# Convolution chain, layer 0: the product of transformed frame 0 comes last and is summed onto the accumulator that VectorE has written in PSUM

## The chip, the core and the metric

The kernel runs on one core of a Trainium2 chip. The metric is the device time of one launch, in microseconds; lower is better. TensorE does the matrix products, VectorE (DVE in the profile) and ScalarE (ACT) do elementwise work, SyncE (SP) issues most transfers. Products land in PSUM; everything else lies in SBUF.

## What is computed

`x` has shape (4, 16, 512, 512). Four layers follow one another, each of the form `x = x + f(groupnorm(x))`. Only layer 0 is touched. Its `f` is a pair of blocks, one after the other, of this kind:

```python
def _denoise_block(x, w1, b1, w2, b2, w3, b3, a, b, c):
    trip = _triplets(x)               # frames t-1, t, t+1, mirrored at the ends
    o = a * conv5x5(trip, w1, dilation 1) + b * conv5x5(trip, w2, dilation 2) + c * conv5x5(trip, w3, dilation 4)
    return jnp.tanh(o)
```

Each of the 16 frames of an image is convolved, in three dilations, together with its two neighbours, and the result goes through tanh. The second block works on the first block's output, and `x` is added at the end. Layers 1 to 3 (a 3x3 convolution of quantised input, a box filter, and a 3x3 convolution in the frequency domain) follow.

## The kernel before

**Groups.** Layer 0 takes four output frames at a time. Along the frame axis it uses a fast convolution: out of six neighbouring input frames `d[0]` to `d[5]` VectorE builds six transformed frames `v[0]` to `v[5]` (128 x 2376 elements each, `early` and `late`), TensorE multiplies each with its own transformed weights, and VectorE combines the six products into four output frames. With 4 images, 2 blocks (`conv` 0 and 1, the outputs are named y and z) and 4 groups a block there are 32 groups. I number them 0 to 31: 0 to 3 are block y of image 0, 4 to 7 block z of image 0, 8 to 11 block y of image 1, and so on.

**Slots.** `run` walks through `slot(n, p)`, six slots p = 0 to 5 for each group n. A slot issues one product (`products`, transformed frame `ORDER[p]`), and everything else that is due beside it. The order of instructions on every engine is the order in which the code issues them; nothing is reordered. In a slot: the weights of the next block are loaded on ACT's queue where the block changes (`load_weights`), then the product, then `gather` for the product of the slot before, then tanh of one finished output frame (`activated`), then `late`, the steps that were put off to this slot (`later`, `do`), the write-out of an output frame (`y_out` or `z_out`), `early` for the next group, and the loads (`fetch`, `input_stats`). `transfers` spreads SP's loads and stores of a slot over the slot's matmuls: each waits for a mark in TensorE's stream.

**PSUM.** A product fills one tile[...], and the pool has two such tiles[...]. Products alternate between them: a product can start only when the readers of the product two slots back are done.

**Gather.** Call the product of `v[q]` M_q. In the order of before, (1, 2, 3, 4, 0, 5):

- at slot 1, ACT copies M1 to tile A; at slot 2, DVE makes B = A - M2 and A = A + M2; at slot 3, ACT copies M3 to C;
- at slot 4, DVE makes D = C - M4, C = C + M4, then for each half E = 4 C + A (output 2, through tanh at once) and A = A + C (L575);
- at slot 5, DVE makes A = A + M0 (L579; output 0), then C = 2 D + B (output 1) and B = 8 D + B;
- at slot 0 of the next group, DVE makes B = B + M5 (L579; output 3), and ACT takes tanh of A; at slot 1, ACT takes tanh of B.

All of these are done in two halves of 128 x 1024 elements. Tiles A to E have one buffer each; E has one half only, so the second E can be written when tanh has read the first. Block z reads its halves out of PSUM with a stride of two elements, block y without one. Output tiles of y come from a pool of two (`rb`), those of z from a pool of two (`ra`) that also holds the normalised input `xp`.

Of the kernel before, what the change touches and what calls it, by code (L numbers as in the profile page):

```python
# [13 lines left out]
F32 = mybir.dt.float32  # L14
AF = mybir.ActivationFunctionType
# [5 lines left out]
P = 128  # L21
B, C, H, W = 4, 16, 512, 512
# [8 lines left out]
DELTA = (-4, -2, -1, 0, 1, 2, 4)  # L31
NPB = 2 * len(DELTA)
NQ = 6
ORDER = (1, 2, 3, 4, 0, 5)
KN = 9 * 264
NFRAMES = 10
AFTER = mybir.DependencyInfo(mybir.DependencyClass.Sync, mybir.DependencyReason.SCHED_ONLY)
# [83 lines left out]
class Layer0:  # L121
# [148 lines left out]
    def first(self):  # L270
# [12 lines left out]
        self.weights()  # L283
        for q in ORDER:
            self.load_weights(0, q)
# [226 lines left out]

    def products(self, gr, p):
        nc, conv, q = self.nc, gr["conv"], ORDER[p]
        ps = self.psum.tile([P, 4, 512], F32, name=f"m{self.now}", tag="m")
        v = gr["v"][q].rearrange("p (k r) -> p k r", r=264 if conv else 72)
        w = self.w[q].rearrange("p (n o) -> p n o", o=PX)
        for n in range(NPB):
            e, dr = n // len(DELTA), DELTA[n % len(DELTA)]
            for turn in range(16):  # L520
                i, j = turn // 4, turn % 4
                rows = slice(PX * i, PX * i + PX)
                r0 = 4 + dr + (64 * j if conv else 0)
                k0 = e + (0 if conv else 8 * j)
                ins = nc.tensor.matmul(  # L525
                    ps[PX * j : PX * j + PX, i, :].rearrange("p (k r) -> p k r", r=64),
                    w[rows, n],
                    v[rows, k0 : k0 + 8, r0 : r0 + 64],
                    start=(n == 0),
                    stop=(n == NPB - 1),  # L530
                    skip_group_check=True,
                )
            self.marks.append(ins.ins)
        gr["m"][q] = ps

    def gather(self, gr, p):

        nc, conv = self.nc, gr["conv"]
        m = gr["m"].pop(ORDER[p])
        s = gr.setdefault("s", {})  # L540

        def new(tag):
            shape = [P, 1024] if tag == "E" else [P, 2, 1024]
            return self.pools["sum"].tile(shape, F32, name=f"{tag}{self.now}", tag=tag)

        def part(h):

            if conv:
                return m.rearrange("p c (k r) -> p (c k) r", r=64)[:, :, h::2]
            return m.rearrange("p c n -> p (c n)")[:, 1024 * h : 1024 * h + 1024]  # L550

        def of(t):
            return t.rearrange("p (k r) -> p k r", r=32) if conv else t

        if p in (0, 2):
            t = s["A" if p == 0 else "C"] = new("A" if p == 0 else "C")
            for h in range(2):
                nc.scalar.copy(of(t[:, h]), part(h))  # L558
        elif p == 1:
            s["B"] = new("B")  # L560
            for h in range(2):
                nc.vector.tensor_sub(of(s["B"][:, h]), of(s["A"][:, h]), part(h))
                nc.vector.tensor_add(of(s["A"][:, h]), of(s["A"][:, h]), part(h))
        elif p == 3:
            s["D"] = new("D")
            for h in range(2):
                c, d = (s[t][:, h] for t in "CD")
                nc.vector.tensor_sub(of(d), of(c), part(h))
                nc.vector.tensor_add(of(c), of(c), part(h))
            for h in range(2):  # L570
                a, c = (s[t][:, h] for t in "AC")
                e = new("E")
                self.stt(e, c, 4.0, a)
                self.activated(gr, 2, h, e)
                nc.vector.tensor_add(a, a, c)  # L575
        else:
            t = s["A" if p == 4 else "B"]
            for h in range(2):
                nc.vector.tensor_add(of(t[:, h]), of(t[:, h]), part(h))  # L579
            for h in range(2) if p == 4 else ():  # L580
                b_, c, d = (s[t][:, h] for t in "BCD")
                self.stt(c, d, 2.0, b_)
                self.stt(b_, d, 8.0, b_)


    def activated(self, gr, i, h, src):

        nc, conv = self.nc, gr["conv"]
        name = f"{gr['b']}_{conv}_{4 * gr['g'] + i}_{h}"
        bias = self.biases[:, conv : conv + 1]  # L590
        if conv:
            z = self.pools["ra"].tile([P, 1024], F32, name=f"z_{name}", tag="ra")
            nc.scalar.activation(z, src, AF.Tanh, bias=bias)
            gr["out"][i, h] = z
        else:
            if h == 0:
                gr["out"][i, 0] = self.pools["rb"].tile([P, 8, 264], F32, name=f"y_{name}", tag="rb")
            z = gr["out"][i, 0]
            o = z[:, :, 4 + 128 * h : 132 + 128 * h].rearrange("p k (c r) -> p c k r", c=2)
            nc.scalar.activation(o, src.rearrange("p (c k r) -> p c k r", c=2, k=8), AF.Tanh, bias=bias)  # L600
            to, even, odd = (
                (z[:, :, 0:4], z[:, :, 8:4:-1], z[:, :, 7:3:-1])
                if h == 0
                else (z[:, :, 260:264], z[:, :, 259:255:-1], z[:, :, 258:254:-1])
            )
            nc.scalar.mul(to, even, self.parity[:, 0:1])
            gr["rim"].append((to, odd))
# [60 lines left out]
    def slot(self, n, p):  # L668

        self.now, self.moves = 6 * n + p, {"first": [], "loads": [], "stores": []}  # L670
        self.marks = []
        groups = self.groups
        cur = groups[n] if 0 <= n < len(groups) else None
        nxt = groups[n + 1] if n + 1 < len(groups) else None
        last = groups[n - 1] if n > 0 else None
        self.last_of_image = (n - 7) % 8 < 2
        if cur:
            if p == 0 and cur["g"] == 0:
                self.begin(cur)
            for i in range(2):  # L680

                if nxt and nxt["g"] and i + 4 in cur["d"]:
                    nxt["d"].setdefault(i, cur["d"][i + 4])

        done, at = (cur, p - 1) if p else (last, 5)
        if done:
            self.free.append(done["v"].pop(ORDER[at]))
            after = nxt if p else cur
            if after and after["conv"] != done["conv"]:
                self.load_weights(after["conv"], ORDER[at])  # L690
        if cur:
            self.products(cur, p)
        if done:
            self.gather(done, at)


        for i, at in enumerate((6, 5, 4, 7)):
            of = cur if p >= 4 or p == 3 and i == 2 else last
            early = of and of["g"] < 3 and i != 3
            if of and of["conv"] and p == (at - early) % 6:  # L700
                of["xb"][i] = [self.load_x(of["b"], 4 * of["g"] + i, h, "xb") for h in range(2)]
        of, i = {4: (cur, 2), 5: (cur, 1), 0: (last, 0), 1: (last, 3)}.get(p, (None, 0))
        if of and i != 2:
            src = of["s"]["CAB"[(1, 0, 3).index(i)]]
            for h in range(2):
                self.activated(of, i, h, src[:, h])
        if cur:
            self.late(cur, p)
        self.do("rows")
        if of:  # L710
            (self.z_out if of["conv"] else self.y_out)(of, i)
        self.do("rest")
        self.do("last")
        if nxt:
            step = p - (3 if nxt["conv"] == 0 and nxt["g"] == 0 else 2)
            if step in (0, 1):
                self.early(nxt, step)
            self.fetch(nxt, p)
        if cur and cur["conv"] == 0 and cur["b"] + 1 < B and p >= 2:
            self.input_stats(cur["b"] + 1, 4 * cur["g"] + p - 2)  # L720
# [66 lines left out]
class Kernel:  # L787
# [594 lines left out]
    def layer3(self, x3, sums, gn, l3, out):  # L1382
# [3 lines left out]
        with ExitStack() as ctx:  # L1386
# [196 lines left out]
            with tc.manual_schedule():  # L1583
# [17 lines left out]
                rows(0)  # L1601
                spread(0)
                products(0)
                imaginary(0)
                load(2)
# [8 lines left out]
                next(edge)  # L1614
                scalars(0)
                products(1)
                next(edge)
                masked(1)
# [101 lines left out]
```

## Time and profile before

| | us |
|---|---|
| median of 3 runs | 5329.93 (5324.8 to 5330.24) |
| the profiled execution | 5314.9 |
| its span | 5313.1 |
| granted TensorE clock, mean of the span | 0.982 |
| layer 0's products (L525), first to last | 74.4 to 3026.6 |

The profiled execution took 1.8 us more than its span, and was 15.0 us faster than the median. The views used are: the page (busy time of each engine, and the span in 40 slices), the groups of instructions by line, the waits (who waited for whom), and the timeline, in which a row has start, duration, engine, line, operation, output and inputs, and in brackets the idle time of the engine before it with what ended it. The profile has 86,016 matmul records in L525. That is 448 for each of the 192 slots, so the start of every 448th record is the start of a slot; slot times below are found that way. The shortest slot takes 14.18 us, the mean one 15.38 us.

### The profile page before, as it was taken

How to read it: one execution, taken by the hardware profiler on the slowest of the kernel's cores; microseconds unless marked ns; L12 is line 12 of the kernel's file. 1: busy time of each engine (PE TensorE's matmuls, PEld its weight loads, DVE VectorE, ACT ScalarE, POOL GpSimd, SP SyncE). 2: the span in 40 equal slices, each digit the busy share in tenths (PEclk: the TensorE clock that was granted, in tenths of full speed). 3: DMA queues.
4: the chain of work that ended last, by engine and by line, in shares of the span. 5: the costliest groups of instructions: out<-in, count | busy, mean ns of one | idle time of the engine just before them, and what ended most of it. 6: DMA issues, size and time to landing. Idle time of an engine off the chain costs nothing.

```text
span 5313.1 us, 270477 instructions
## 1 busy us (share of the span) xinstructions
PE 5014.8 (94%) x125040; PEld 3651.4 (69%) x125040; DVE 4034.6 (76%) x4764; ACT 2491.1 (47%) x3954; POOL 6.8 (0%) x20
## 2 busy tenths in 40 slices
PE   4999998999999999989999789998999989999999
PEld 3676676766776856758766655566887867777776
DVE  7867989768988669987689855555555578888887
ACT  2543445533255533444122445554454446666665
POOL 0000000000000000000000000000000000000000
PEclk9999999999999999999999999999999989999999
DMA  5555554555545455543346377776666655555554
GB/s 170 170 145 157 144 156 148 161 148 137 143 152 169 139 160 137 150 134 117 103 128 153 126 222 231 234 238 202 225 222 199 214 158 143 144 149 148 143 143 121
DMA packets 445356, 861.49 MB, mean 162 GB/s; under 512 B 74304, under 2 KB 96704, under 8 KB 443968
## 3 DMA queue, kind: packets, MB, share of 16 engines
q1 hardware_dynamic: 415792, 797.68, 51.8%
q10 hardware_dynamic: 28432, 46.52, 2.7%
q8 instruction: 979, 16.04, 1.4%
q14 instruction: 153, 1.25, 0.1%
HBM read 503.87 MB, written 340.03 MB: 159 GB/s over the span
## 4 chain that ended last, share of the span: by engine, by line
PE 89%; DVE 6%; issue 2%; DMA 2%; ACT 1%; SPq 0%; ACTq 0%; POOL 0%; DVEq 0%; POOLq 0%
PE m L525 51%; PE l1p L975 10%; PE l2p L1082 8%; PE u L1550 4%; PE s L1491 4%; PE u L1491 4%; PE u L1513 2%; PE pt L1525 2%; DVE l2o L1122 2%; PE l2p L1133 1%; DVE st L1123 1%; DVE frame L441 0%; PE pr L1535 0%; ACT xp L377 0%; DVE zr L627 0%
## 5 line engine op out<-in xcount | busy, mean ns | idle before, releaser
L525 PE MATMUL m<-frame,l0w 32*32 32x512 f32 x86016 | 2856.1, 604 | 170.5 <-DVE frame L481 74.4
L525 PEld LDWEIGHTS m<-frame,l0w 32*32 32x32 f32 x86016 | 2073.7, 103 | 952.0 <-issue 363.1
L441 DVE SCALAR_TENSOR_TENSOR frame<-frame,frame 128x2376 f32<-128x2376 f32 x232 | 607.9, 2629 | 9.2 <-DMA xs<-in_x 0.8
L975 PE MATMUL l1p<-l1q,l_wt 32*32 32x512 f32 x12288 | 482.6, 600 | 61.3 <-DVE l1q L965 35.7
L975 PEld LDWEIGHTS l1p<-l1q,l_wt 32*32 32x32 f32 x12288 | 258.3, 103 | 231.6 <-issue 155.4
L1122 DVE TENSOR_TENSOR l2o<-l2x,l2p 128x512 f32<-128x512 f32 x256 | 172.7, 675 | 270.4 <-PE l2p L1082 270.4
L652 ACT ACTIVATE junk<-xb,neg 128x1024 f32<-128x1024 f32 x256 | 294.2, 1149 | 62.1 <-DMA l0w<-l0w 32.9
L1082 PEld LDWEIGHTS l2p<-k_c_band,l2y 128*128 128x128 f32 x2048 | 256.8, 190 | 76.0 <-issue 55.2
L1082 PE MATMUL l2p<-k_c_band,l2y 128*128 128x144 f32 (+1 forms) x2048 | 284.3, 292 | 6.1
L1082 PE MATMUL l2p<-k_c_band,l2n 128*128 128x144 f32 (+1 forms) x2048 | 272.5, 294 | 14.4 <-ACT l2n L1100 10.9
L1111 ACT COPY l2y<-l2p 128x512 f32<-128x512 f32 x256 | 149.9, 586 | 286.9 <-PE l2p L1082 286.9
L1082 PEld LDWEIGHTS l2p<-k_c_band,l2n 128*128 128x128 f32 x2048 | 265.8, 199 | 15.3 <-ACT l2n L1100 11.4
L992 DVE BATCH_NORM_STATS2 l1st<-l1o 128x6 f32<-128x512 f32 x256 | 158.2, 681 | 140.3 <-ACT l1o L990 140.3
L990 ACT ACTIVATE l1o<-l1p,k_l_bias,l_osc 128x1024 f32<-128x1024 f32 x128 | 147.2, 1201 | 240.1 <-PE l1p L975 234.2
L1550 PE MATMUL u<-k_c_hil,zt 128*128 128x128 f32 x2048 | 255.9, 278 | 0.0
L558 ACT COPY C<-m 128x1024 f32<-128x1024 f32 x64 | 61.6, 1014 | 405.9 <-PE m L525 317.6
L1550 PEld LDWEIGHTS u<-k_c_hil,zt 128*128 128x128 f32 x2048 | 238.4, 192 | 2.1 <-issue 0.8
L405 DVE STREAM_TRANSPOSE frame<-xp 128x1056 f32<-128x1056 f32 x128 | 162.8, 1282 | 90.5 <-ACT xp L379 90.4
L1526 ACT COPY zt<-pt 128x512 f32<-128x512 f32 x256 | 131.4, 599 | 207.8 <-PE pt L1525 207.8
L1456 DVE TENSOR_TENSOR xc<-l3n,k_c_tab 128x2048 f32<-128x2048 f32 x64 | 146.7, 2292 | 108.1 <-ACT l3n L1440 108.1
L1569 DVE SCALAR_TENSOR_TENSOR l3o<-u,l3t 128x256 f32<-128x256 f32 x512 | 192.3, 427 | 22.3 <-ACT l3t L1561 19.5
L975 PE MATMUL l1p<-l1x,l_wt 32*32 32x512 f32 x4088 | 196.7, 597 | 0.0
(309 smaller groups left out, 6376.9 us busy)
## 6 DMA issues: line engine op xcount, KB each, us to landing
y<-y SPq DMA_DIRECT2D x256, 264.0 KB
frame<-y SPq DMA_DIRECT2D x512, 132.0 KB
x<-l1o SPq DMA_DIRECT2D x256, 256.0 KB
l2x<-x SPq DMA_DIRECT2D x64, 1024.0 KB
x<-l2o SPq DMA_DIRECT2D x64, 1024.0 KB
l3x<-x SPq DMA_DIRECT2D x256, 256.0 KB
out<-l3o SPq DMA_DIRECT2D x256, 256.0 KB
l1x<-x SPq DMA_DIRECT2D x252, 256.0 KB
```

Source lines behind the costliest of these rows:

```text
L405: nc.vector.transpose(v[:, :, 4 + h : 68 : 2], xp)
L441: self.nc.vector.scalar_tensor_tensor(o, x, f, y, ALU.mult, ALU.add)
L525: ins = nc.tensor.matmul(ps[PX * j : PX * j + PX, i, :].rearrange("p (k r) -> p k r", r=64), w[rows, n], v[rows, k0 : k0 + 8, r0 : r0 + 64 ...
L652: nc.scalar.activation(junk, xs[h], f, bias=neg, accum_out=self.out_sums[n][:, 2 * t + h : 2 * t + h + 1])
L975: ins = nc.tensor.matmul(ps[32 * j : 32 * j + 32, b, :], wt[rows, a, d], qs[v % 3][rows, k, d : d + W] if d < 3 else raws[v][rows, k], sta ...
L992: nc.vector.bn_stats(st[b][:, u, :], o[:, b, :])
L1082: nc.tensor.matmul(ps[:, lo:hi], lhs[:, k, at : at + P], band[:, j : j + hi - lo], start=(k == 0), stop=(k == 3), skip_group_check=True,)
L1111: nc.scalar.copy(yts[i][:, wb, :], ps)
L1122: nc.vector.tensor_add(o[:, hb, :], xt[:, hb, :], ps)
L1491: nc.tensor.matmul(ps[b][32 * j : 32 * j + 32], f[rows, n, j, :], x[rows, j, :], start=(i == 0), stop=(i == 2 and tag == "s"), skip_group_ ...
L1550: nc.tensor.matmul(po[:, bass.ts(k, P)], zt[:, b, k ^ 1, :], hil[:, k, :], start=False, stop=(k == 3), skip_group_check=True,)
L1569: nc.vector.scalar_tensor_tensor(o[:, v].rearrange("p k u -> p u k"), po[:, HW:W].rearrange("p (u k) -> p u k", u=2), s, t.rearrange("p (u ...
```

## The change

Frame 0 and frame 5 change places: the order is (1, 2, 3, 4, 5, 0).

- At slot 4, a PSUM tile `base` is taken (the one that M4 has just been read from), and DVE writes A + C into it, both halves, before the two E steps. The SBUF-only step A = A + C goes.
- At slot 5, TensorE adds the product of `v[0]` to that tile: no matmul of this product has `start`. DVE gathers M5 in this slot, for each half after C = 2 D + B and B = 8 D + B.
- At slot 0 of the next group DVE gathers nothing. ACT takes tanh of output 0 straight from PSUM.

```diff
-ORDER = (1, 2, 3, 4, 0, 5)
+ORDER = (1, 2, 3, 4, 5, 0)
...
-        ps = self.psum.tile([P, 4, 512], F32, name=f"m{self.now}", tag="m")
+
+        ps = gr.pop("base") if q == 0 else self.psum.tile([P, 4, 512], F32, name=f"m{self.now}", tag="m")
...
-                    start=(n == 0),
+                    start=(n == 0 and q != 0),
...
-        def part(h):
+        def part(h, m=m):
...
+            base = gr["base"] = self.psum.tile([P, 4, 512], F32, name=f"m{self.now + 1}", tag="m")
+            for h in range(2):
+                a, c = (s[t][:, h] for t in "AC")
+                nc.vector.tensor_add(part(h, base), of(a), of(c))
             for h in range(2):
                 a, c = (s[t][:, h] for t in "AC")
                 e = new("E")
                 self.stt(e, c, 4.0, a)
                 self.activated(gr, 2, h, e)
-                nc.vector.tensor_add(a, a, c)
-        else:
-            t = s["A" if p == 4 else "B"]
+        elif p == 4:
             for h in range(2):
-                nc.vector.tensor_add(of(t[:, h]), of(t[:, h]), part(h))
-            for h in range(2) if p == 4 else ():
                 b_, c, d = (s[t][:, h] for t in "BCD")
                 self.stt(c, d, 2.0, b_)
                 self.stt(b_, d, 8.0, b_)
+                nc.vector.tensor_add(of(b_), of(b_), part(h))
+        else:
+            s["M"] = [part(h) for h in range(2)]
...
-            nc.scalar.activation(z, src, AF.Tanh, bias=bias)
+            to = z.rearrange("p (k r) -> p k r", r=32) if i == 0 else z
+            nc.scalar.activation(to, src, AF.Tanh, bias=bias)
...
-            src = of["s"]["CAB"[(1, 0, 3).index(i)]]
+            src = of["s"]["CMB"[(1, 0, 3).index(i)]]
             for h in range(2):
-                self.activated(of, i, h, src[:, h])
+                self.activated(of, i, h, src[h] if i == 0 else src[:, h])
```

## The prediction

> **What bounds the kernel now.** I read the page first, then the waits of TensorE inside layer 0, then DVE's groups, then the timeline at the slots where TensorE waits.
>
> ```profile
> PE 5014.8 (94%) x125040; PEld 3651.4 (69%) x125040; DVE 4034.6 (76%) x4764; ACT 2491.1 (47%) x3954; POOL 6.8 (0%) x20
> ...
> PE   4999998999999999989999789998999989999999
> ...
> DVE  7867989768988669987689855555555578888887
> ```
>
> ```profile
> PE m L525 <- DVE frame L481: 74.4, 1, 74.4
> PE m L525 <- issue: 68.7, 40, 10.8
> PE m L525 <- ACT C L558: 13.0, 5, 5.4
> PE m L525 <- DVE frame L441: 9.3, 5, 4.4
> PE m L525 <- PE m L525: 3.4, 5, 0.9
> ```
>
> TensorE bounds layer 0: its row is nines from slice 2 on, and after the first 74.4 us it waits only 94.4 us in total (68.7 + 13.0 + 9.3 + 3.4). That is the most that lighter DVE work could give back. In its 2953 us DVE is busy for 2400, so work taken from it counts only where TensorE is waiting for it.
>
> ```profile
> L575 DVE TENSOR_TENSOR A<-A,C 128x1024 f32<-128x1024 f32 x64 | 78.4, 1225 | 2.2
> ...
> L568 DVE TENSOR_TENSOR D<-C,m 128x1024 f32<-128x1024 f32 x64 | 77.8, 1215 | 17.3 <-PE m L525 17.3
> ...
> L579 DVE TENSOR_TENSOR B<-B,m 128x1024 f32<-128x1024 f32 x62 | 72.5, 1210 | 39.0 <-PE m L525 38.9
> ```
>
> These are the steps that the change drops, turns into PSUM writes, or moves. The timelines show where DVE holds TensorE (DVE's rows, then TensorE's):
>
> ```profile
> 808.74 2.34 DVE L579 TENSOR_TENSOR A<-A,m 128x1024 f32<-128x1024 f32 x2
> ...
> 826.17 2.31 DVE L579 TENSOR_TENSOR B<-B,m 128x1024 f32<-128x1024 f32 x2
> ...
> 866.55 2.63 DVE L441 SCALAR_TENSOR_TENSOR frame<-frame,frame 128x2376 f32<-128x2376 f32 x1
> ...
> 899.93 1.22 DVE L569 TENSOR_TENSOR C<-C,m 128x1024 f32<-128x1024 f32 x1
> ```
>
> ```profile
> 811.18 1.17 PE L525 MATMUL m<-frame,l0w 32*32 32x512 f32 x16 [4.71 <-issue]
> ...
> 869.28 5.32 PE L525 MATMUL m<-frame,l0w 32*32 32x512 f32 x102 [10.52 <-issue]
> ...
> 901.26 19.35 PE L525 MATMUL m<-frame,l0w 32*32 32x512 f32 x592 [0.95 <-PE m L525]
> ```
>
> The waits marked "issue" are DVE's in truth. TensorE goes on at 811.18, 0.10 us after A + M0 has ended (group 7, so group 8 can start); at 869.28, 0.10 us after frame `v[4]` of group 8; at 901.26, 0.11 us after the last C + M4 of group 8, which frees the tile for slot 5. From 780 to 905 us, between two images, DVE has hardly a gap. The same places return in images 2 and 3.
>
> ```profile
> 1420.26 0.01 DVE L433 LOAD_MASK_SELECT frame<-frame  x1 [3.13 <-DMA frame<-y]
> ...
> 1438.01 1.22 DVE L569 TENSOR_TENSOR C<-C,m 128x1024 f32<-128x1024 f32 x1
> 1439.15 1.22 DVE L441 SCALAR_TENSOR_TENSOR E<-C,A 128x1024 f32<-128x1024 f32 x1
> 1440.40 1.22 DVE L575 TENSOR_TENSOR A<-A,C 128x1024 f32<-128x1024 f32 x1
> 1441.59 1.23 DVE L441 SCALAR_TENSOR_TENSOR E<-C,A 128x1024 f32<-128x1024 f32 x1
> ```
>
> This is slot 4 of group 14, in the middle of an image. The slot began at 1424.3; DVE came to C + M4 so late because in slot 3 it had waited for a load, not because it had too much to do. It ends at 1439.23, and slot 5 starts at 1439.45: a margin of 0.2 us.
>
> **The change part by part.**
>
> DVE's sum. A = A + C becomes the write of `base`: two steps for two. No row shows a DVE write to PSUM. The nearest are SBUF to SBUF (1225 ns, L575) and PSUM read (1215 ns, L568), the latter with z's stride and without it alike (L562: 9.69 us for the 8 steps of block z of image 0, 9.71 for those of block y of image 1), so the read side costs nothing. [...] I take 1225 ns, 2.45 us for both[...]. B = B + M5 moves from slot 0 to slot 5, and A = A + M0 is gone: 2 x 1.21 = 2.43 us less for a group, 78 us over 32. But E has one half. In before, A + C (1.23 us) lay between the two E steps and covered tanh of the first (1.15 us). Now the second E waits for tanh: about 1.2 us of idle DVE for a group. Net: some 1.2 us less for a z group, and about nothing for a y group, where the second rim step also waits for a tanh that A + C had covered.
>
> New wait at slot 5. TensorE's slot 5 needed the last C + M4; now it needs `base` 2.45 us later. Queued behind the waiting matmul is all of TensorE. Taking for each group the time from the end of C to the start of slot 5, most have 3 us or more and pay nothing. These do not: group 0 (0.10), 8, 16, 24 (0.10 each), 13 (1.78), 14 (0.20), 21 (1.35), 22 (1.62), 27 (0.23), 30 (2.45), and 7, 15, 23 (0.10). The price is 2.45 + 0.10 less the margin. Groups 13, 14, 21, 22, 30: 0.77 + 2.35 + 1.20 + 0.93 + 0.10 = 5.35 us. Group 27: 2.32 us. DVE was late there because of a load, as in the lines above, so the step saved at slot 0 earns no credit: 7.7 us.
>
> Between the images. Group 7: slot 5 starts 2.3 us later. Then the release of M5's tile comes after C, B, add, C, B, add (7.3 us) instead of after two adds (2.34), and the E wait puts DVE 1.1 us later: group 8 starts near 817.2 instead of 811.2. Next, slot 1 of group 8 needs the tile that tanh of output 0 reads; ACT ended that in before at 833.95, 5.4 us after the slot had begun, and I get 835.3 against 828.6. So TensorE is 6.7 us late here. It does not last: slot 3 of group 8 is set by DVE's frame at 869.18, and slots 1 and 2 end by 864.6. DVE's own chain there is +1.2 - 2.3 with a little ACT: 0.9 us earlier. SP's loads are tied to marks of TensorE, but at 836 to 871 SP is behind those marks already, held by buffers. At slot 5 of group 8 the `base` steps add 2.45; the 0.9 comes off if it passes ScalarE's wait for an input load at 870 us (0.72 us). I take 2.0 us a boundary, three times: 6.0 us.
>
> First group: slot 5 waits 2.45 us more, group 1's first two slots shift by more, and the frame that ends at 218.6 collects it; going down DVE's rows with the input statistics and the y store in between I get 1.6 us.
>
> Last group. B + M5 (2.35 us from 3026.61) goes from between the last product and layer 1, and tanh of output 0 (2.17 us) runs beside DVE's output steps: 2.35 us less.
>
> Restart. [...] This case: after waits of 5 us and more, and after one of 2.52 (773.57), the next slot has two steps of 0.74 us at matmuls 16 and 32 and costs 1.4 us; after others of 2.51 and 3.1 it doesn't. [...] I take one, 1.4 us.
>
> At nothing: tanh from PSUM (ACT's copy from PSUM takes 1014 ns, tanh from SBUF 1150; if it were slower, ACT is idle several us in every slot). Tile use of slot 1: outside group 0 and the boundaries tanh of output 0 ended 3.7 us or more before it. Release for slot 0: its margin is 5 us or more against some 6, of which slot 5's own delay gives back the rest. Weight loads on ACT's queue and frames freed keep their slots. If these covers were gone, each would cost the shortfall, under 2 us a place.
>
> Sum: 7.7 + 6.0 + 1.6 - 2.35 + 1.4 = 14.3 us; 5314.9 becomes 5329.2, and the median 5329.93 becomes 5344.
>
> **The rivals.** A measurement of this kernel can tell about 0.2%, 10.7 us, from no change.
>
> Absorbed: TensorE's short gaps inside slots (some 130 us above 14.2 us a slot outside the slot borders) shrink after a stall, and half of the new waits vanish: about 5334. For it: those gaps are irregular. Against: nothing shows that a stall fills them.
>
> Boundary not absorbed: SP's loads do follow the 6.7 us, and slot 3 of group 8 with them. 3 x 6.7 on top gives 5364. It decides once SP is no longer behind the marks.
>
> Relief counts: DVE is the bound between images, the dropped add (2.43 us) goes through to slot 5 of groups 8, 16 and 24, cancels `base` there and shortens three boundaries, the start and the end; and `base` finds slack. 5 x 2.4 = 12 us less: 5318. For it: DVE's unbroken rows from 780 to 905. Against: margins of 0.1 to 0.2 us at slot 5, and the E wait. It decides only if DVE's lateness at slot 4 is carried over from slot 0; the 3.13 us wait for a load says no.
>
> [...]
>
> **How the numbers follow.** New wait, 5344: 0.50, of which 0.10 falls inside the bound; not absorbed 0.16; absorbed 0.24; relief 0.10. Slower 0.40 + 0.16 = 0.56, same 0.34, faster 0.10. The range, 5328 to 5363, takes in absorbed, most of the slower case and the unknown write price; the likeliest case's own is 5337 to 5353.
>
> **What would show it.** `base` near 1.22 us a half; the second E waiting about 1.2 us for tanh; TensorE waiting for `base` at slot 5 of groups 14 and 27; group 8 starting some 6 us later and its slot 3 at the same place or earlier; the last product about 15 us later, and layer 1 some 2 us closer to it. Slot 3 of group 8 several us earlier, or no wait at slot 5, would prove me wrong.

## The result, and the profile after

| | before | after |
|---|---|---|
| median of 5 runs, us | 5329.93 (5324.8 to 5330.24) | 5350.48 (5341.12 to 5357.6) |
| profiled execution, us | 5314.9 | 5341.12 |
| its span, us | 5313.1 | 5339.3 |
| granted TensorE clock, mean | 0.982 | 0.98 |

The ratio is 1.0043, 95% interval 1.0028 to 1.0058: 20.5 us slower by the medians, where the prediction said 14.3. Both profiles are fast draws, before's by 15.0 us under its median and after's by 9.4, so their difference of 26.2 us is some 6 too large. A second session with the same kernel (below) gave 1.0040 [1.0023, 1.0057].

First the page of after, busy time and slices:

```profile
PE 5022.7 (94%) x125040; PEld 3689.4 (69%) x125040; DVE 3970.0 (74%) x4700; ACT 2485.1 (47%) x3954; POOL 6.9 (0%) x20
...
PE   4999998999999999989999889998999989999999
...
DVE  7866979767888858988578856555555578888887
```

DVE has 64 instructions and 64.6 us less to do; TensorE has as many instructions as before (125,040). The groups of DVE say what the new step and E cost (total, duration of one in ns, then the idle time before them):

```profile
L574 DVE TENSOR_TENSOR m<-A,C 128x1024 f32<-128x1024 f32 x64 | 78.9, 1233 | 2.2
L441 DVE SCALAR_TENSOR_TENSOR E<-C,A 128x1024 f32<-128x1024 f32 x64 | 78.2, 1222 | 38.9 <-ACT y L605 19.5 <-ACT z L598 19.4
```

The write of `base` (L574) takes 1233 ns a half. The second E waits 38.9 us in 32 groups, 1.22 each: that is what the dropped A = A + C had covered.

TensorE's waits inside layer 0 (engine and line, who was waited for; us in total, times, longest):

```profile
PE m L526 <- DVE frame L481: 74.9, 1, 74.9
PE m L526 <- issue: 67.8, 44, 8.0
PE m L526 <- DVE m L574: 17.9, 6, 4.4
PE m L526 <- ACT C L559: 17.5, 6, 5.1
PE m L526 <- ACT y L605: 4.4, 1, 4.4
PE m L526 <- ACT z L598: 3.2, 3, 1.6
PE m L526 <- DVE frame L441: 1.3, 1, 1.3
```

After the first wait these are 112.1 us, against 94.4 before. The row "DVE m L574" is new: six waits for `base`. It does not hold all of the waits for `base`: some still stand under "issue". Here is one from the new row, in the middle of an image, at slot 5 of group 5 (DVE's rows, then TensorE's):

```profile
613.58 1.22 DVE L570 TENSOR_TENSOR C<-C,m 128x1024 f32<-128x1024 f32 x1
614.83 2.50 DVE L574 TENSOR_TENSOR m<-A,C 128x1024 f32<-128x1024 f32 x2
617.24 1.22 DVE L441 SCALAR_TENSOR_TENSOR E<-C,A 128x1024 f32<-128x1024 f32 x1
619.67 1.23 DVE L441 SCALAR_TENSOR_TENSOR E<-C,A 128x1024 f32<-128x1024 f32 x1 [1.22 <-ACT z L598]
```

```profile
599.45 14.19 PE L526 MATMUL m<-frame,l0w 32*32 32x512 f32 x415
617.48 28.12 PE L526 MATMUL m<-frame,l0w 32*32 32x512 f32 x783 [3.84 <-DVE m L574]
```

The last C ends at 614.80. In before no later step stands in the way of slot 5; now TensorE goes at 617.48, 0.15 us after `base` (614.83 + 2.50).

Between images 0 and 1, TensorE in the timeline of after (slot 5 of group 7, slot 0 of group 8, slots 1 and 2; then slot 3, and slot 5 of group 8):

```profile
806.54 17.03 PE L526 MATMUL m<-frame,l0w 32*32 32x512 f32 x448 [4.42 <-DVE m L574]
831.14 16.78 PE L526 MATMUL m<-frame,l0w 32*32 32x512 f32 x448 [7.57 <-issue]
848.93 29.67 PE L526 MATMUL m<-frame,l0w 32*32 32x512 f32 x896 [1.01 <-ACT z L598]
882.19 10.12 PE L526 MATMUL m<-frame,l0w 32*32 32x512 f32 x244 [3.59 <-issue]
...
918.68 31.91 PE L526 MATMUL m<-frame,l0w 32*32 32x512 f32 x916 [3.56 <-issue]
```

TensorE's lag behind before, read slot by slot, each kernel counted from its own first matmul, is 12.9 us when slot 4 of group 7 starts, 15.7 at its slot 5, 19.5 when group 8 starts, 12.4 at its slot 3 (where before waited 10.5 us for the frame, and after 3.6), 16.9 at its slot 5, and 19.1 when group 9 starts. Most of this growth lies in waits. The last part, 2.2 us, is no wait: slot 5 of group 8 itself takes 16.39 us instead of 14.23. The windows of time show why. First before, in the first 3.4 us of slot 5 of groups 7 and 8, then after at the same two slots (window, its length, PE busy and matmuls, granted clock, DMA share, GB/s):

```profile
790.40:793.80 3.40, 3.40 (x109) 1.00 0.90 209
901.26:904.66 3.40, 3.40 (x111) 1.00 0.14 39
```

```profile
806.54:809.94 3.40, 3.40 (x65) 0.50 0.06 22
918.68:922.08 3.40, 3.40 (x65) 0.50 0.00 0
```

After waits of 4.4 and 3.6 us the clock is granted at 0.50, and 65 matmuls are issued in the time of 110. I call this a slow start, or a restart. A slot that starts so is over a microsecond longer, beyond the wait itself.

### The profile page after: what moved, and what is told of

The parts are those of the page before. It is cut to its first block, busy times and chain, and to the rows that moved or that the text cites. A ratio compares the mean times of both kernels' runs of the same rounds, so it can differ in the third digit from the quotient of the medians.

```text
span 5339.3 us, 270467 instructions
## 1 busy us (share of the span) xinstructions
PE 5022.7 (94%) x125040; PEld 3689.4 (69%) x125040; DVE 3970.0 (74%) x4700; ACT 2485.1 (47%) x3954; POOL 6.9 (0%) x20
## 4 chain that ended last, share of the span: by engine, by line
PE 86%; DVE 7%; issue 2%; DMA 2%; ACT 2%; SPq 0%; ACTq 0%; DVEq 0%; POOL 0%; POOLq 0%
PE m L526 49%; PE l1p L980 10%; PE l2p L1087 7%; PE u L1555 4%; PE s L1496 4%; PE u L1496 4%; PE u L1518 2%; PE pt L1530 2%; DVE l2o L1127 2%; PE l2p L1138 1%; DVE frame L441 1%; DVE st L1128 1%; ACT xp L377 0%; PE pr L1540 0%; DVE frame L481 0%
## 5 line engine op out<-in xcount | busy, mean ns | idle before, releaser
L526 PEld LDWEIGHTS m<-frame,l0w 32*32 32x32 f32 x86016 | 2118.3, 103 | 937.1 <-issue 368.3
L1087 PE MATMUL l2p<-k_c_band,l2n 128*128 128x144 f32 (+1 forms) x2048 | 267.8, 291 | 14.0 <-ACT l2n L1105 10.5
L441 DVE SCALAR_TENSOR_TENSOR y<-y,k_c_parity 128x32 f32<-128x32 f32 x128 | 30.5, 249 | 260.7 <-ACT y L611 222.5
```

What stands on the lines that cost most here:

```text
L441: self.nc.vector.scalar_tensor_tensor(o, x, f, y, ALU.mult, ALU.add)
L526: ins = nc.tensor.matmul(ps[PX * j : PX * j + PX, i, :].rearrange("p (k r) -> p k r", r=64), w[rows, n], v[rows, k0 : k0 + 8, r0 : r0 + 64 ...
L1087: nc.tensor.matmul(ps[:, lo:hi], lhs[:, k, at : at + P], band[:, j : j + hi - lo], start=(k == 0), stop=(k == 3), skip_group_check=True,)
```

## What a wait costs beside itself

All 14 profiles of this case together (before, after and the twelve experiments) have 2674 slot starts. I sorted them by the gap from the start of the last matmul of one slot to the start of the first of the next (some 0.6 us more than the idle time in a row's brackets), and measured the time of the first 64 matmuls. The last column counts the slots in which the granted clock was below full speed during these 64:

| gap before the slot, us | slots | first 64 matmuls, median us | slots over 2.8 us | slots with a lowered clock |
|---|---|---|---|---|
| under 1 | 2296 | 2.09 | 51 | 0 |
| 1 to 2 | 84 | 1.77 | 0 | 1 |
| 2 to 3 | 77 | 2.14 | 25 | 41 |
| 3 to 4 | 60 | 2.92 | 32 | 51 |
| over 4 | 157 | 3.38 | 147 | 157 |

A gap of over 4 us costs 1.3 us more, nearly always; one of 2 to 4 us does so in 57 of 137 cases; one of 1 to 2 us does not. The 204 slow starts behind gaps of over 1 us ran at a mean clock of 0.50 to 0.60. The 51 slots over 2.8 us behind gaps under 1 us ran at full clock, so they have another cause and are not counted below.

In the traces the same wait costs a restart in one execution and none in the next, and this goes with where the wait falls. In each of the 14 profiles all stretches at half clock in layer 0, 12 to 24 of them (12 in before and 21 in after, the one in front of layer 1 counted), start on one grid of 3.413 us, to within 5 ns, and where this grid lies against the kernel's start differs from execution to execution. The clock was lowered behind none of the 98 gaps of over 1 us that cover less than 1.7 us of any one step of this grid, behind 34 of the 63 that cover 1.7 to 2.2 us, and behind 216 of the 217 that cover more. A gap of 2 to 4 us can fall on either side of that.

Slow starts behind gaps of over 1 us number 9 in before and 17 in after, and together they cost 11.2 and 20.2 us over the 2.09. So the account of the lag at the end of layer 0, 29.2 us, is: gaps between slots 95.3 to 115.4, +20.1; slow starts +9.0; the rest, inside slots, +0.1. In the repeated run it is 24.3 us: gaps +24.0, slow starts +11.7 (19 of them), rest -11.4. The rest scatters between executions of whatever kernel, so that it came to 0.1 in the first profile is chance. Before itself has only one profile: 9 is one draw. Layer 1 then takes back 3.2 us (4.9 in the repeat), as its own first wait shows, before and then after:

```profile
3062.24 1.88 PE L975 MATMUL l1p<-l1q,l_wt 32*32 32x512 f32 x2 [35.67 <-DVE l1q L965]
```

```profile
3088.68 1.88 PE L980 MATMUL l1p<-l1q,l_wt 32*32 32x512 f32 x2 [32.44 <-DVE l1q L970]
```

## Experiments

Each session timed its kernels beside before on one chip; chips differ between sessions. Ratios are to before; medians differ by some tenths of a per cent between sessions (before's lie between 5299.94 and 5333.45), so only ratios and differences in one session count, and a difference in us is given as the ratio's share of before's median. The same holds for the absolute times in the expectations: they start from before at 5330. Edits are shortened; "..." stands for lines left out. "Slot-5 waits" are the gaps before slot 5 summed over the 25 groups away from the image ends (0, 7, 8, 15, 16, 23 and 24 left out); in before they are 0, in after 9.3 us.

**The order alone.** Frame 0 last and M5 gathered early, but no seed (no sum that is written into PSUM ahead of the product): A = A + C stays in SBUF and DVE adds M0 at slot 0. The edit is against after.

```diff
+    start=(n == 0)
...
-    base = gr["base"] = self.psum.tile(...)
-    for h in range(2):
-        nc.vector.tensor_add(part(h, base), of(a), of(c))
...
+        nc.vector.tensor_add(a, a, c)
...
-            s["M"] = [part(h) for h in range(2)]
+            nc.vector.tensor_add(of(A), of(A), part(h))
```

> The new order of the six products stays, and so does the late gather of M5 (C, B, add for each half), but nothing is seeded in PSUM: A = A + C is made in SBUF in its old place, M0 goes to a tile of its own and VectorE adds it to A at slot 0. Theory 1 (the cost is the write of base that stands between the gather of M4 and slot 5): slot 5 again waits for C + M4 only, so about 5330 us, at most 5 us more for the later release of M5's tile. Rival (the new order itself, with the later release before slot 0): it keeps its cost, about 5350 us.

Measured: 5328.24 against 5321.69, ratio 1.0009 [0.9997, 1.0021]. Slot-5 waits 2.3 us. The order costs some 5 us, not told from nothing: most of the loss lies in the seed.

**The write alone.** Before, with `base` written into slot 5's tile (here that of M5), and then overwritten because this product keeps its `start`.

```diff
+    base = gr["base"] = self.psum.tile(...)
+    for h in range(2):
+        nc.vector.tensor_add(part(h, base), of(a), of(c))
...
+    ps = gr.pop("base") if p == 5 else self.psum.tile(...)
```

> The kernel before, with one thing added: after the gather of M4, VectorE writes A + C into the PSUM tile of slot 5's product, which then overwrites it (its first matmuls have start). Order, gather, tanh and everything else are those of before; VectorE has 2.46 us more work for a group. Theory 1: the wait at slot 5 is all there is to it, so some 15 to 22 us more than before, 5345 to 5352 us. Rival (late release, second E step waiting for tanh): neither is here, so 5330 us, or as much more as 2.46 us of VectorE work cost between the images (three times, 7 us).

Measured: 5360.87 against 5321.69, ratio 1.0077 [1.0059, 1.0095]: +41 us, twice what I expected. Gaps between slots are 27.4 us more than before (slot 5 in mid-image groups 17.6, the groups at the image ends 10.5), and slow starts 16 instead of 9 (+8.3 us). Two of its waits, the second in front of layer 1:

```profile
PE m L525 <- issue: 92.3, 51, 10.7
PE l1p L979 <- DVE l1q L969: 37.8, 1, 37.8
```

It is also some 19 us slower than after (1.0043 and 1.0040; the intervals just miss each other), although the same write stands in front of slot 5. The difference is what after saves: A = A + C and A = A + M0, 4.9 us of DVE a group, less the E wait, with the order changed besides. Where these steps count can be seen. From the start of group 7 to that of group 9, and likewise at the other two image boundaries, this kernel falls 22.2 us further behind before, after only 14.3 (12.9 in the repeat). At slot 3 of groups 8, 16 and 24 it is still 3.0 to 4.1 us late, where after is between 2.3 us early and 0.5 late. And layer 1's wait is 2.1 us longer than in before, where after's is 3.2 shorter. So after's +21 us is a net: a larger cost at slot 5, less a relief of DVE at the image ends.

**Both, so that the place differs.** After with A = A + C kept (its result unused), one step behind each E.

```diff
     self.activated(gr, 2, h, e)
+    nc.vector.tensor_add(a, a, c)
```

> The changed kernel, with A = A + C left in its old place behind each E step (its result is used by nobody). VectorE has 2.45 us more work for a group, as much as before the change, of which 1.2 us fill the idle time at the second E step. Theory 1: relief of VectorE is worth next to nothing, so 5350 us, at most 4 us more (1.2 us at three boundaries). Rival (the relief does earn some 10 us, which the wait at slot 5 hides): about 5360 us.

Measured: 5350.27, ratio 1.0051 [1.0033, 1.0068], +27 us. DVE has as many steps a group here as in the order-alone kernel, and the E steps don't wait (idle before them 0.0). Between the two, +5 and +27, lie 22 us for having two of these steps in front of slot 5 instead of behind it. To after (+21) the difference is within the intervals, so this run does not decide between the two expectations for the relief (20 to 24 us over before, or 30).

**The write twice.** After with `base` written two times.

```diff
     for h in range(2):
         nc.vector.tensor_add(part(h, base), of(a), of(c))
+    for h in range(2):
+        nc.vector.tensor_add(part(h, base), of(a), of(c))
```

> The changed kernel, with base written twice over (four steps instead of two, the same values). Slot 5 can start 2.46 us later. Theory 1, by the margins of the changed kernel: the twelve groups that wait for base outside the last group of an image (0, 5, 6, 8, 13, 14, 16, 21, 22, 24, 27, 29) pay 2.46 us more each, 29.5 us, and the eight y groups with 0.7 to 1.1 us of margin left (1, 2, 9, 10, 17, 18, 25, 26) begin to pay 1.4 to 1.8 us each, 12 us: some 40 us more than the changed kernel, 5380 to 5395 us. Rival (VectorE's total load or the late release): 2.46 us more for a group between the images only, 5355 to 5360 us.

Measured: 5380.09 against 5302.0, ratio 1.0143 [1.0126, 1.0161]: +76 us, 55 over after in the same session. The waits of TensorE:

```profile
PE m L526 <- DVE frame L481: 75.4, 1, 75.4
PE m L526 <- issue: 74.4, 37, 9.4
PE m L526 <- DVE m L577: 57.8, 20, 6.8
```

The row of `base` goes from 6 waits to 20, and slot-5 waits in mid-image groups from 17.7 us (repeat) to 52.2. All eight y groups that were named beforehand (1, 2, 9, 10, 17, 18, 25 and 26) now wait, by gaps of 1.3 to 1.9 us where 1.4 to 1.8 were expected. The path is confirmed. The second write cost 55 us where some 40 were expected. It saves nothing, so it stands beside the 41 of the write alone, and not beside after's net of 21; whether it costs more than the first, the intervals don't tell.

**After once more**, in the same session.

> The changed kernel once more, on the chip of the two others, to compare them with it: 5345 to 5355 us.

Measured: 5321.66 against 5302.0, ratio 1.0040 [1.0023, 1.0057]. Slot-5 waits in mid-image groups were 17.7 us in this profile, in groups 5, 13, 14, 21, 22, 29 and 30; in the first profile 9.3, in 5, 6, 21 and 22.

**Filling slot 4.** After with C = 2 D + B and B = 8 D + B taken from slot 5 to slot 4, behind each E, so that they cover the wait for tanh and M5's tile is free after two adds.

```diff
     self.activated(gr, 2, h, e)
-elif p == 4:
-    for h in range(2):
         b_, c, d = (s[t][:, h] for t in "BCD")
         self.stt(c, d, 2.0, b_)
         self.stt(b_, d, 8.0, b_)
-        nc.vector.tensor_add(of(b_), of(b_), part(h))
+elif p == 4:
+    for h in range(2):
+        nc.vector.tensor_add(of(s["B"][:, h]), of(s["B"][:, h]), part(h))
```

> The changed kernel, with C = 2 D + B and B = 8 D + B moved up into slot 4, each right behind the E step of its half. The second E step no longer leaves VectorE idle for 1.2 us, and the gather of M5 is two adds, so its tile comes free 4.9 us earlier than in the changed kernel. The write of base is where it was. Theory 1: slot 5 waits as in the changed kernel; group 8 and its like start about 5 us earlier, which slot 3 takes back; the idle time saved is worth at most 1.2 us a boundary. About 5345 us, 5340 to 5351. Rival (late release and idle E step are the cost): about 5330 us.

Measured: 5329.92 against 5321.69, ratio 1.0020 [1.0010, 1.0030], +11 us. The 5330 that the rival named is met only as an absolute time, in a session in which before took 5321.69; as a difference, the theory gave 10 to 21 us and the rival none, so +11 lies at the theory's lower end and off the rival. The idle time before E is gone:

```profile
L441 DVE SCALAR_TENSOR_TENSOR E<-C,A 128x1024 f32<-128x1024 f32 x64 | 78.0, 1219 | 0.0
```

Two more kernels split the edit, and it was repeated beside them. In the first the same steps stand behind both E steps, so E still waits; in the second only the first half's C = 2 D + B stands between the E steps, so M5's tile is still released late.

```diff
     for h in range(2):
         self.stt(e, c, 4.0, a)
         self.activated(gr, 2, h, e)
+    for h in range(2):
+        self.stt(c, d, 2.0, b_)
+        self.stt(b_, d, 8.0, b_)
...
```

> The changed kernel with the two C and two B steps of a group (4.9 us of DVE) taken from behind the products of frame 5 to the end of slot 4, behind both E steps: M5's tile is released after two adds again, but the second E still waits about 1.2 us for tanh. e3_fill, where the same steps lay between the two E steps, cost +10.6 us against before, the changed kernel +21. If the late release made the difference: as e3_fill, +8 to +13 us (about 5332). If the idle 1.2 us in each group made it: near the changed kernel, +17 to +22 us.

```diff
     self.activated(gr, 2, h, e)
+    if h == 0:
+        self.stt(c, d, 2.0, b_)
...
```

> The changed kernel with only the first half's C step moved between the two E steps, so that the wait of the second E for tanh is covered, while the release of M5's tile still comes after five steps (B, add, C, B, add; 6.1 us instead of 7.3). If the idle E step made the difference between e3_fill and the changed kernel: +9 to +13 us against before. If the late release made it: +17 to +22 us. If both count for half: about +15 us.

> e3_fill once more, beside the two kernels that split its edit: the ratio to before was 1.0020 [1.0010, 1.0030]. Both theories expect the same again, 1.001 to 1.003, that is +5 to +16 us; in its second profile the waits of TensorE at slot 5 in mid-image groups (1.7 us in the first) should stay under 5 us if filling slot 4 takes them away.

Measured against 5299.94 in one session: early release 5319.55, 1.0039 [1.0028, 1.0050]; wait filled 5316.9, 1.0037 [1.0024, 1.0049]; both together again 5314.16, 1.0026 [1.0015, 1.0036]. Each half was expected to bring the +11 if it was the cause, and neither shows a gain alone over after's 1.0040. Both together gave 1.0020 and 1.0026; some 7 to 11 us of after's cost may lie there, but the intervals touch, and which of the two does it stays open. The slot-5 waits of the filled kernel were 2.1 us in the first profile and 15.0 in the second, so the reading of the first one, that filling slot 4 takes them away, was the draw of one execution.

**The seed only in the last group of a block z** (7, 15, 23, 31), with the filled slot 4; all other groups as before.

```diff
+SEEDED = (1, 2, 3, 4, 5, 0)
...
-    {"b": b, "conv": conv, "g": g, ...}
+    {"order": SEEDED if conv and g == 3 else ORDER, "b": b, "conv": conv, "g": g, ...}
```

> A version meant to keep the gain and drop the cost: only the last group of block z of each image (groups 7, 15, 23, 31) has the new order and the seed, with C and B moved up behind the E steps; the other 28 groups are those of before. In those four groups the wait at slot 5 is taken back by slot 3 of the next group (or falls before layer 1). Theory 1: no new wait that lasts, VectorE 2.4 us earlier at slot 3 of groups 8, 16 and 24 where slot 5 of that group doesn't give it back, and the last product 2 to 3 us closer to layer 1: 5320 to 5328 us. Rival (the relief never passes ScalarE's waits between the images): 5327 to 5331 us, the same as before.

Measured: 5298.11 against 5302.0, ratio 0.9986 [0.9977, 0.9995]. It was run again, and beside it the same without the seed (order and moved steps kept, A = A + C in SBUF, M0 added by DVE):

> e6_last_group once more: its ratio was 0.9986 [0.9977, 0.9995]. If seeding the last group alone is a gain, again 0.998 to 0.9995, that is -3 to -10 us; if it was the scatter of one session, 0.9995 to 1.001.

> e6_last_group (which took 7.4 us off) without its seed: in groups 7, 15, 23 and 31 frame 0 comes last and the C and B steps stand in slot 4, but A = A + C is made in SBUF and DVE adds M0 at the next slot 0. If e6's gain is the work that DVE no longer does at image ends (M0's add, 2.4 us a group, four groups): 0 us, ratio 0.999 to 1.001. If it is the order and the earlier steps: -5 to -9 us as e6, ratio 0.998 to 0.9992.

Measured against 5333.45: with the seed 5324.34, 0.9986 [0.9978, 0.9995]; without it 5332.85, 1.0001 [0.9992, 1.0011]. So where DVE is what the next work waits for, at the end of an image and in front of layer 1, taking M0's add from it is worth 0.14%, some 7 us, and this version is faster than both kernels. The wait in front of layer 1 shows part of it, without the seed and then with it:

```profile
3066.86 1.88 PE L985 MATMUL l1p<-l1q,l_wt 32*32 32x512 f32 x2 [35.31 <-DVE l1q L975]
```

```profile
3067.84 1.88 PE L994 MATMUL l1p<-l1q,l_wt 32*32 32x512 f32 x2 [32.20 <-DVE l1q L984]
```

That is 3.1 us. The other 4 or so are not placed: over the three image boundaries the two seeded profiles take 5.3 and -0.7 us, the unseeded one -0.2.

## Why the prediction was right, and which terms were off

Slower, by 20.5 us in place of 14.3, inside the range given for the likeliest case. The mechanism is shown: without the seed the loss goes (+5, not told from nothing), with the write alone it comes (+41), with the write doubled it grows (+76). The profiles agree: from layer 0's first matmul to layer 1's first they take 1.3, 41.4 and 79.1 us more than before's, and after's 25.9 and 19.4; the unchanged part behind scatters by up to 19 us. By the prediction's steps:

- **The price of the write.** Taken at 1225 ns; 1233 measured, y and z alike (the longest of the 64 is 1234). That is 8 ns above L575, which writes SBUF. Over the thirteen places at slot 5 that the prediction lists, two halves each, it comes to 0.2 us; nothing hangs on that.
- **E's wait.** Said 1.2 us a group; 1.22.
- **Slot 5 in the middle of images.** Said 7.7 us, in groups 13, 14, 21, 22, 30 and 27. Measured 9.3 and 17.7 us. In the repeat five of the named groups waited (13, 14, 21, 22, 30), with 5 and 29 besides; in the first profile 21 and 22, with 5 and 6; group 27 in neither. The mechanism holds, but one profile of before does not say which of the z groups will be late. In 12 z groups of each of the 14 profiles, DVE begins slot 4 between 14.1 and 14.9 us after its wait for a load in slot 3 (in all but one, which had no such wait); so a margin there depends on when the load arrives, and that differs between executions. The sum over groups was near, the list was not. Over the seven profiles of kernels that have the seed in all groups and one write (9.3, 17.7, 2.1, 15.0, 7.2, 15.2, 12.2) the mean is 11.2; over the three without a seed in any group (before, the order alone and the unseeded last group: 0, 2.3, 1.3) it is 1.2.
- **The image boundary.** Group 8 was said to start some 6.0 us later and slot 1 of group 8 to be 6.7 us late; measured against the start of group 7, 6.1 and 6.5. By slot 3 this was to be absorbed but for -0.9, and the lag there is 12.4, 0.9 below the 13.3 at the start of group 7. The exact hit is luck: at the other two boundaries and in the repeat it is between -2.3 and +0.5. SP's loads did not follow the shift: three that start at 847 to 859 us in before come 12.1 to 13.5 us later in after, counted like the lag: as group 7 does, and not 19.5. That rules out "boundary not absorbed". But the boundary as a whole took 5.7, 6.7 and 1.9 us (start of group 7 to start of group 9, and likewise), 14.3 for the three, in place of 6.0. The gaps between slots in groups 7, 8, 15, 16, 23 and 24 grew from 71.8 to 78.2 us, 6.4, about the forecast (in the repeat 3.1); most of the other half is the next point: after gaps of over 1 us the first 64 matmuls of these groups took, over the 2.09, 5.5 us more in sum than in before (repeat 8.6).
- **Clock restarts: the term that was most too small.** The prediction took one, 1.4 us; the number of them was its author's estimate. Measured: 8 more slow starts in after than in before, +9.0 us, and 10 more in the repeat, +11.7. Against the three unseeded kernels (9, 12 and 10 slow starts, on average 12.9 us) the seven seeded ones (14 to 19, on average 19.1 us) have 6.2 us more, and this is the better figure. Slot 5 of groups 0, 5, 6, 7, 8, 16 and 24 are among them in the first profile, seven where the sum has one. Two of its own numbers, 2.52 us with and 3.1 without a restart, were draws from the middle rows of the table above. The clock was lowered after 41 of 77 gaps of 2 to 3 us, and behind 34 of the 63 gaps that cover 1.7 to 2.2 us of a step of the grid above. So every slot 5 that waits for more than 2 us should have carried a share of a restart.
- **First group and tail.** Said +1.6 and -2.35; the first two groups took 2.4 and 1.4 us in the two profiles, and layer 1 came 3.2 and 4.9 us closer.
- **The relief.** The rival "relief counts" was right about a place and wrong about the sum. At image ends and in front of layer 1 DVE's saved steps are worth something: 7 us by the seed in the last groups alone, and some 19 between the write alone and after. With the seed in all groups slot 5 outweighs it. In the forecast it stood at -0.9 us a boundary and -2.35 at the end.
- **Absorbed.** Steps of over 0.3 us between matmuls inside slots sum to 139 us in before and to between 119 and 155 in the others, in no order with the waits. Nothing shows that a stall fills them.

So the terms that were too small are the restarts, by some 5 us on average, and the waits in mid-image groups, by some 2; the tail gave back over 1 us more than was said (layer 1's wait is 3.0 to 4.9 us shorter than in before in the seven seeded profiles, and up to 0.6 in the unseeded ones). With these averages the sum is about 20. Single profiles scatter by ten us and more in these terms, so the averages show that the sizes fit and do not prove each one; that the first forecast came within 6 us is in part luck.

## What to carry to other kernels

A step saved on an engine that is not the bound is not worth its own length; ask where that engine holds the next work, and in front of which wait the remaining steps now stand. Here 64.6 us of DVE work went and was seen to count only between images and in front of layer 1, and the 2.45 us moved in front of TensorE's last slot cost more; used only where DVE holds the next work, the same edit pays. When a change lengthens TensorE's waits, count each wait that grows past 2 us with the chance of a slow start of 1.3 us more (here 57 of 137 gaps of 2 to 4 us and 147 of 157 longer ones), and treat margins that depend on a transfer as chances, to be summed over all groups, not as a list read from one execution.

## What I had not expected of the hardware

Tanh of output 0 is a little faster when it reads PSUM than when it reads SBUF. From PSUM it took 1092 to 1129 ns in block y and 1107 to 1118 in z, where the read has a stride of two elements; from SBUF, in before, 1132 to 1158 and 1132 to 1153. A DVE write to PSUM costs the same with z's stride of two elements as without (1232 to 1234 ns over all 64). And after a gap of 1 to 2 us the first 64 matmuls of a slot are faster, 1.77 us in place of 2.09; the cause was not tested.
